# A first attention in one kernel with three other layers: transposes behind a step's four products, finishing in small pieces, value products two steps behind

## The chip, the core and the metric

One NeuronCore of a Trainium2 chip runs the whole program. Its engines work side by side, each through its own instruction stream in order: TensorE (PE: matmuls, and transposes as matmuls with an identity), VectorE (DVE), ScalarE (ACT: exponentials and copies), GpSimd (POOL) and SyncE, which starts DMAs. Products land in PSUM, from where DVE or ACT must read them. The metric is device time in microseconds: the median of the kernel's runs, 1323.51 us over three (1322.59 to 1324.91).

## The reference

Four layers follow each other on x of 1024 tokens x 256 channels, all in fp32. Each is wrapped the same way: layer norm before, layer norm behind, then added to x. Only the first, an attention of 16 heads of 16 channels, is touched.

```python
def _L0_attn_ref(X, ln_w, ln_b, W_in, W_out):
    ...
    Q, K = (_rope(Q), _rope(K))
    scores = jnp.einsum('bhqd,bhkd->bhqk', Q, K) / jnp.sqrt(jnp.float32(Dh))
    probs = jax.nn.softmax(scores, axis=-1)
    ctx = jnp.einsum('bhqk,bhkd->bhqd', probs, V)
    ctx = ctx.transpose(0, 2, 1, 3).reshape(B, S, D)
    out = jnp.einsum('bsd,df->bsf', ctx, W_out)
    return out + X
...
x = L0_attn_X
x = x + _layernorm(_L0_attn_ref(_layernorm(x, axis=-1), ...), axis=-1)
x = x + _layernorm(_L0_ffn_ref(_layernorm(x, axis=-1), ...), axis=-1)
```

The second layer is a mixture of 8 experts; a second attention and a mixture of 16 experts follow.

## The kernel before

**Tiling.** Heads come in four groups g of four; a head has a slot of 32 partitions, so the four heads of a group lie in the four 32-row strips of TensorE. Queries are taken in two halves qh of 512 tokens. The eight pairs (qh, g) are `steps`, numbered n = 0 to 7. An fp32 product runs as two passes, so every product shows as two matmul instructions.

**Two passes over the scores.** `largest` computes for every n the scores with queries in rows (L396) and reduces them on DVE to a maximum for each query and head (L401), which is written into the queries as an extra channel (L415). It has 16 positions s per n: half of the keys, a tile of 128 queries, a pair of heads. `attend(qh, g)` then computes the scores with keys in rows (L443), which come out with the maximum subtracted, takes the exponential on ACT (L472) into tiles `pe` (six buffers), and multiplies them with the values (`gather`, L437) into `po`, which has one PSUM buffer. It has eight key tiles st; each is done in two half-steps of two heads.

**How they are woven together.** `largest` and `attend` are generators. `attend` yields once in a half-step, after its first score and before its second; there the caller pulls one position of `largest`: two products, for the two heads that `attend` is not using. So the four products of a half-step lie in four row strips. After them comes half of a value product: four heads, 256 of 512 columns, of the key tile before (st - 1). In the first tile of an attend there is none; tile 0's values are taken whole at the end of tile 1, and the last tile's whole at the end of the attend, followed by an ACT copy of `po` to `oT` (L479). All score tiles, and everything that is transposed or projected, share one PSUM ring of seven buffers, tag b1. A tile waits until the one seven places earlier has been read.

**Transposes.** `turned` (L354, L355) makes four 128x128 transposes and an ACT copy. `largest` calls it at fixed positions: at s = 1 for the signed queries of n - 1 (`signed`), at s = 9 and 11 for the next group's keys (n + 1 < 4 only), at s = 13 for the next unsigned queries (`unsigned`), and at the end for the last signed queries. As it is called inside `largest`, it runs in the middle of the half-step, between `attend`'s first and second score. `pull(2 * TT + 2)` runs 18 positions ahead of the first attend, and one half-step (n = 0, i = 7) pulls three at once. So `largest` ends after 54 of the 64 key tiles. The last ten run "alone": four scores at once, four exponentials (L461), a whole value product.

**Finishing.** When n = 4 begins, the first half of the queries is finished by `finished(0)`, one step at every yield, again in the middle of a half-step: four `by_token` (four transposes L492, a reciprocal and a multiplication on DVE), two `by_channel` (transposes L507, ACT copy), two `projected` (eight matmuls L517, then on DVE L524 and all of `turn_over`: statistics, the scale with its power on POOL L184, the addition to x, statistics and scale again, then `h` on ACT L206). `turn_over` leaves `turned`, which transposes `h` (L216) and copies it to `hT` (L217), two yields later. The second half of the queries is finished by the same functions between the gates of the experts that follow (`experts0`, whose matmuls are L645). Those read `hT` of the first half of the tokens first.

The order written in the code is not fully binding: the framework may put an instruction that is ready ahead of one that is not.

Of the kernel before, what the change touches and what calls it, by code (L numbers as in the profile page):

```python
# [23 lines left out]
H = 16  # L24
# [25 lines left out]
class Net:  # L50
# [139 lines left out]

    def turn_over(self, ps, tts):

        nc = self.nc
        tp = tts[0] // 2
        xs = self.pair(self.x, tp)
        rs, nb = self.scales(self.pair(self.acc, tp))
        for i, x in enumerate(xs):
            nc.vector.scalar_tensor_tensor(  # L200
                x, self.acc[:, 2 * tp + i, :], rs[:, i : i + 1], x, ALU.mult, ALU.add
            )
        rs2, nb2 = self.scales(xs)
        h = self.row.tile([P, 2, D], F32, tag="h2", name="h")
        for i, x in enumerate(xs):
            nc.scalar.activation(  # L206
                h[:, i, :], x, AF.Identity, scale=rs2[:, i : i + 1], bias=nb2[:, i : i + 1]
            )
        for i, x in enumerate(xs):
            nc.gpsimd.tensor_scalar(x, x, nb[:, i : i + 1], None, ALU.add)  # L210

        def turned(ps):
            pt = ps.tile([P, KC, 2, P], F32, tag="b1", name="pt")
            for i in range(2):
                for k in range(KC):
                    nc.tensor.transpose(pt[:, k, i, :], h[:, i, k * P : (k + 1) * P], self.ident)  # L216
            nc.scalar.copy(  # L217
                self.hT[:, :, 2 * tp * P : (2 * tp + 2) * P], pt.rearrange("p k i t -> p k (i t)")
            )

        self.todo.extend([None, None, turned])
# [103 lines left out]
    def attention0(self):  # L325
# [4 lines left out]
        with ExitStack() as ctx:  # L330
# [49 lines left out]
            def largest(first):  # L380
# [6 lines left out]
                for n, (qh, g) in enumerate(steps):  # L387
                    raw = raws.pop(n)
                    pm = self.small.tile([P, QT, G, 2], F32, tag="pm", bufs=2, name="pm")
                    for s, (kh, tt, pair) in enumerate(order):  # L390
# [13 lines left out]
                        if s % 2 == 1:  # L404
                            next(first, None)
                        if n > 0 and s == 1:
                            signed(n - 1)
                        if n + 1 < len(steps):
                            nqh, ng = steps[n + 1]
                            if nqh == 0 and s in (9, 11):  # L410
                                turned(kT[:, ng, half((s - 9) // 2)], ng, 1, (s - 9) // 2)
                            if s == 13:
                                unsigned(n + 1)
                        if s == len(order) - 1:
                            nc.vector.tensor_reduce(  # L415
                                qk[:, qh * QT : (qh + 1) * QT, 0, g * G : (g + 1) * G, DH : DH + 1],
                                pm, AX.X, ALU.max, negate=True,
                            )
                            if n == len(steps) - 1:
                                signed(n)  # L420
                        yield

            def attend(qh, g, alone):


                qm = ready.pop((qh, g))
                po = pso.tile([P, HALF], F32, tag="po", name="po")
                NQ = HALF // 2

                def gather(st, pe, quarter, whole=False):  # L430
                    c = slice(quarter * NQ, (quarter + 1) * NQ)
                    if st == 0 or whole:
                        if quarter == 0:
                            return
                        c = slice(0, HALF)
                    for j in range(G):
                        nc.tensor.matmul(  # L437
                            po[rows(j), c], va[:, st, g * G + j, :], pe[j // 2][:, j % 2, c],
                            start=(st == 0), stop=(st == TT - 1 and quarter == 1),
                        )  # L440
# [8 lines left out]
                before = None  # L449
                for st in range(TT):  # L450
                    pe = [pp.tile([P, 2, HALF], F32, tag="pe", name="pe") for _ in range(G // 2)]
                    pairs = list(reversed(range(G // 2)))
                    if alone():

                        scs = []
                        for pair in pairs:
                            for i in range(2):
                                scs.append((pair, i, ps.tile([P, HALF], F32, tag="b1", name="sc")))
                                score(scs[-1][2], st, 2 * pair + i)
                        for pair, i, sc in scs:  # L460
                            nc.scalar.activation(pe[pair][:, i, :], sc, AF.Exp, scale=scale)  # L461
                        if before is not None:
                            gather(st - 1, before, 1, True)
                        before = pe
                        yield
                        yield
                        continue
                    for at, pair in enumerate(pairs):
                        for i in range(2):
# [3 lines left out]
                            if i == 0:  # L473
                                yield
                        if before is not None:
                            gather(st - 1, before, at)
                    before = pe
                gather(TT - 1, before, 1, True)
                nc.scalar.copy(oT[:, g, half(qh)], po)  # L479

            def finished(qh):
# [4 lines left out]
                def by_token(tp, i, ps):  # L486
                    if i == 0:
                        cxs[tp] = self.row.tile([P, 2, H, DH], F32, tag="h2", name="cx")
                    tt = 2 * tp + i
                    pt = ps.tile([P, H, SLOT], F32, tag="b1", name="pt")  # L490
                    for g in range(NG):
                        nc.tensor.transpose(  # L492
                            pt[:, g * G : (g + 1) * G, :].rearrange("p h c -> p (h c)"),
                            oT[:, g, tt * P : (tt + 1) * P], self.ident,
                        )
                    rec = self.small.tile([P, H, 1], F32, tag="rec", name="rec")
                    nc.vector.reciprocal(rec, pt[:, :, DH : DH + 1])
                    nc.vector.tensor_tensor(
                        cxs[tp][:, i, :, :], pt[:, :, 0:DH], rec.to_broadcast([P, H, DH]), ALU.mult
                    )  # L500

                def by_channel(tp, ps):
                    cx = cxs[tp].rearrange("p i h c -> p i (h c)")
                    pc = ps.tile([P, KC, 2, P], F32, tag="b1", name="pc")
                    for i in range(2):
                        for k in range(KC):
                            nc.tensor.transpose(pc[:, k, i, :], cx[:, i, k * P : (k + 1) * P], self.ident)  # L507
                    cT = self.row.tile([P, KC, 2, P], F32, tag="cT", bufs=2, name="cT")
                    nc.scalar.copy(cT, pc)
                    cxs[tp] = cT  # L510

                def projected(tp, ps):
                    cT = cxs.pop(tp)
                    po = ps.tile([P, 2, D], F32, tag="b1", name="po")
                    for i in range(2):
                        for k in range(KC):
                            nc.tensor.matmul(  # L517
                                po[:, i, :], cT[:, k, i, :], self.w_out[:, k, :],
                                start=(k == 0), stop=(k == KC - 1),
                            )  # L520

                    for i in range(2):
                        tt = 2 * tp + i
                        nc.vector.scalar_tensor_tensor(  # L524
                            self.acc[:, tt, :], self.x[:, tt, :], self.rs0[:, tt : tt + 1],
                            po[:, i, :], ALU.mult, ALU.add,
                        )
                    self.turn_over(ps, [2 * tp, 2 * tp + 1])

                for tp in tps:  # L530
                    for i in range(2):
                        yield lambda ps, tp=tp, i=i: by_token(tp, i, ps)
                for tp in tps:
                    yield lambda ps, tp=tp: by_channel(tp, ps)
                for tp in tps:
                    yield lambda ps, tp=tp: projected(tp, ps)
# [19 lines left out]
            left = [2 * TT * len(steps)]  # L556
            ahead = largest(beside())

            def pull(n):
                for _ in range(n):  # L560
                    if left[0]:
                        next(ahead)
                        left[0] -= 1

            pull(2 * TT + 2)
            after = iter(())
            for n, (qh, g) in enumerate(steps):
                if n == NG:
                    after = finished(0)
                for i, _ in enumerate(attend(qh, g, lambda: left[0] == 0)):  # L570
                    pull(3 if n == 0 and i == 7 else 1)
                    step = next(after, None)
                    if step is not None:
                        step(ps)
                    else:
                        self.catch_up(ps, 1)
            for step in after:
                step(ps)
            self.catch_up(ps, len(self.todo))
# [740 lines left out]
```

## Time and profile before

| | |
|---|---|
| median of 3 runs | 1323.51 us |
| profiled execution, its own time | 1320.31 us |
| its span, first to last instruction | 1318.5 us |
| PE busy, share of span | 94% |
| DVE, ACT, POOL busy | 55%, 38%, 11% |
| mean granted PE clock | 0.986 |
| from the first score of attend 0 to the first matmul of the experts | 69.53 to 339.06 us |

The page divides the span among engines and lists groups of instructions by source line; the trace behind it gives every instruction's start and duration. "Idle before" names whose end ended a wait. PE's busy share says little, because the passes of up to four products run at the same time in different row strips, and the end of a matmul is modelled. What counts here is the distance from one start to the next. The granted clock says at which share of its full speed PE ran.

### The profile page before, as it was taken

To read this page: it belongs to the slowest core of one execution; us is meant where nothing else is said; L and a number is where in the kernel's file an instruction comes from. 1 tells how busy PE (TensorE), PEld (TensorE's weight loads), DVE (VectorE), ACT (ScalarE), POOL (GpSimd) and SP (SyncE) were. 2 spreads that over 40 slices of the span, in tenths; PEclk is the share of its full clock that TensorE was granted. 3 is DMA by queue.
4 is the path that set the end of the run, shared out by engine and by line. 5 is a ranking of instruction groups with operands and counts; after the bars stand their busy time and mean duration, and the time that the engine had idled before them with its cause. 6 is when DMAs were issued, how large, how long until landed. Compare 5 with 4: busy or idle time off the path is not lost. (4 is left out here: it accounts for less than half of the span.)

```text
span 1318.5 us, 15710 instructions
## 1 busy us (share of the span) xinstructions
PE 1244.9 (94%) x6088; PEld 729.0 (55%) x6088; DVE 731.6 (55%) x1657; ACT 497.4 (38%) x911; POOL 149.4 (11%) x137
## 2 busy tenths in 40 slices
PE   5899999999999998889999999999998799999997
PEld 2433333332456565456676767676767456655655
DVE  4675665563243335777586777777775633233334
ACT  3256663566441111454545444445445122011111
POOL 2100000100010002111212121211112400000000
PEclk9999999899999999899999999999999899999999
DMA  6000000000005101200212112130211103723000
GB/s 189 1 1 1 1 1 1 0 1 1 1 1 172 53 12 53 83 33 32 72 33 72 50 56 72 33 103 33 73 32 34 61 1 95 218 80 108 32 25 32
DMA packets 38923, 64.42 MB, mean 49 GB/s; under 512 B 4776, under 2 KB 28552, under 8 KB 38848
## 3 DMA queue, kind: packets, MB, share of 16 engines
q1 hardware_dynamic: 38848, 63.41, 15.2%
q8 instruction: 48, 0.79, 0.3%
q14 instruction: 27, 0.22, 0.1%
HBM read 62.12 MB, written 1.28 MB: 48 GB/s over the span
## 5 line engine op out<-in xcount | busy, mean ns | idle before, releaser
L401 DVE TENSOR_REDUCE pm<-sc 128x1 f32<-128x512 f32 x256 | 163.4, 684 | 94.2 <-PE sc L443 56.5
L443 PE MATMUL sc<-qTm,kT 32*128 32x512 f32 x512 | 170.5, 644 | 2.4 <-DVE pm L401 1.7
L648 DVE TENSOR_TENSOR mid<-sg,pu 128x512 f32<-128x512 f32 (+1 forms) x82 | 56.4, 687 | 200.3 <-PE pu L645 166.7
L472 ACT ACTIVATE pe<-sc 128x512 f32<-128x512 f32 x216 | 119.1, 595 | 87.5 <-PE sc L443 59.3
L647 ACT ACTIVATE sg<-pg 128x512 f32<-128x512 f32 (+1 forms) x82 | 48.9, 596 | 270.2 <-PE pg L645 270.0
L396 PE MATMUL sc<-kT,qT 32*128 32x512 f32 x512 | 140.1, 643 | 1.7 <-ACT qT L355 1.1
L969 ACT ACTIVATE sn<-pt,shift,rs 128x128 f32<-128x128 f32 x256 | 93.6, 470 | 106.9 <-DVE shift L965 106.8
L929 PE MATMUL px<-hT,w_l1a 128*128 128x512 f32 x256 | 124.1, 597 | 4.1 <-issue 3.5
L921 DVE SCALAR_TENSOR_TENSOR y<-px,cp,y 128x1023 f32<-128x1023 f32 (+5 forms) x102 | 123.2, 1211 | 2.5 <-ACT y L915 2.5
L184 POOL TENSOR_TENSOR rs<-ve,nhalf 128x2 f32<-128x2 f32 (+1 forms) x29 | 20.8, 717 | 702.6 <-DVE ve L183 698.1
L645 PE MATMUL pg<-hT,w_l1f 128*128 128x512 f32 (+1 forms) x200 | 96.0, 603 | 0.7 <-ACT hT L217 0.7
L671 DVE TENSOR_TENSOR acc<-acc,po 128x512 f32<-128x512 f32 (+1 forms) x61 | 41.1, 674 | 99.7 <-PE po L663 99.7
L645 PE MATMUL pu<-hT,w_l1f 128*128 128x512 f32 (+1 forms) x200 | 94.6, 595 | 0.0
L663 PE MATMUL po<-w_l1f,mid 128*128 128x256 f32 (+1 forms) x400 | 87.5, 379 | 0.0
L443 PEld LDWEIGHTS sc<-qTm,kT 32*128 32x128 f32 x512 | 52.5, 185 | 63.2 <-issue 42.0
L964 POOL TENSOR_TENSOR rs<-ve,nhalf 128x8 f32<-128x8 f32 x32 | 52.4, 1638 | 299.5 <-DVE ve L963 244.7
L437 PE MATMUL po<-pe,va 128*32 128x256 f32 (+1 forms) x832 | 83.3, 444 | 1.9 <-ACT pe L461 1.2
L663 PEld LDWEIGHTS po<-w_l1f,mid 128*128 128x128 f32 (+1 forms) x400 | 76.0, 190 | 13.4 <-issue 3.3
L1063 PE MATMUL pg<-hT,w_l1a 128*128 128x512 f32 x128 | 61.9, 609 | 6.5 <-DVE og L1145 4.8
L645 PEld LDWEIGHTS pu<-hT,w_l1f 128*128 128x128 f32 (+1 forms) x200 | 38.2, 191 | 48.9 <-issue 48.7
L437 PEld LDWEIGHTS po<-pe,va 128*32 128x32 f32 x832 | 18.3, 108 | 84.6 <-issue 63.7
L645 PEld LDWEIGHTS pg<-hT,w_l1f 128*128 128x128 f32 (+1 forms) x200 | 37.9, 192 | 44.7 <-issue 43.3
(196 smaller groups left out, 1936.1 us busy)
## 6 DMA issues: line engine op xcount, KB each, us to landing
spread<-rows SPq DMA_DIRECT2D x32, 512.0 KB, 4.5
w<-w SPq DMA_DIRECT2D x16, 512.0 KB, 5.0
w_l1f<-in_e_gT SPq DMA_DIRECT2D x4, 640.0 KB, 4.0
w_l1f<-in_e_uT SPq DMA_DIRECT2D x4, 640.0 KB, 5.3
w_l1f<-in_e_dT SPq DMA_DIRECT2D x4, 640.0 KB, 7.2
w_l0f<-in_e_wg SPq DMA_DIRECT2D x4, 512.0 KB, 3.7
w_l0f<-in_e_wu SPq DMA_DIRECT2D x4, 512.0 KB, 5.8
w_l0f<-in_e_wd SPq DMA_DIRECT2D x4, 512.0 KB, 6.7
```

The lines of the kernel that those rows point to most:

```text
L396: nc.tensor.matmul(sc, raw[r, tt * P : (tt + 1) * P], kT[r, g, half(kh)], start=True, stop=True,)
L401: nc.vector.tensor_reduce(pm[:, tt, 2 * pair + i, kh : kh + 1], sc, AX.X, ALU.max)
L437: nc.tensor.matmul(po[rows(j), c], va[:, st, g * G + j, :], pe[j // 2][:, j % 2, c], start=(st == 0), stop=(st == TT - 1 and quarter == 1),)
L443: nc.tensor.matmul(sc, kT[rows(j), g, st * P : (st + 1) * P], qm[rows(j), :], start=True, stop=True,)
L472: nc.scalar.activation(pe[pair][:, i, :], sc, AF.Exp, scale=scale)
L645: nc.tensor.matmul(p, w(k), self.hT[:, k, c], start=(k == 0), stop=(k == KC - 1))
L648: nc.vector.tensor_tensor(mid, sg, pu, ALU.mult)
L663: nc.tensor.matmul(po[:, i, :], left[:, at * P : (at + 1) * P], right, start=(n == 0), stop=(n == len(pieces) - 1),)
L921: nc.vector.scalar_tensor_tensor(y[:, at:hi], px[:, at - j : hi - j], column(cw + 4 * h + 3 - j), y[:, at:hi], ALU.mult, ALU.add,)
L929: nc.tensor.matmul(px[:, c], w[:, k, hh * DK : (hh + 1) * DK], self.hT[:, k, c], start=(k == 0), stop=(k == KC - 1),)
L969: nc.scalar.activation(sn[:, n, :], pts[n // 4][:, n % 4, :], AF.Identity, scale=rs[:, n : n + 1], bias=shift[:, n : n + 1],)
L1063: nc.tensor.matmul(pg, wg[:, k, hh * DK : (hh + 1) * DK], self.hT[:, k, c], start=(k == 0), stop=(k == KC - 1),)
```

## The change

Three things change in the first attention. A pull now returns what is to be transposed instead of doing it, and the caller runs it at the end of the half-step, behind the second score and the value product. The value products go into a list `sums` that outlives an attend: a half-step takes one entry while more than two are in it, so that they run two key tiles behind, across the borders between attends. Tile 0's whole product takes two entries, the first of them empty. The finishing of the first query half becomes a generator of small pieces, `finished_slowly` with `turn_over_slowly`, advanced once at the end of every half-step, from seven half-steps into n = 4 on. The pull of three at once is gone; 20 positions are pulled ahead of the first attend. `finished(1)` stays, but its projection now takes the two token tiles one after the other, each followed by its DVE instruction.

```diff
+    def turn_over_slowly(self, ps, tp, acc):
...
+        mv = small("mv", 2)
+        for i in range(2):
+            acc(i)
+            yield
+            stats(mv, i, accs[i])
+            yield
+        rs, nb = scale(mv)
+        yield
+        mv = small("mv", 2)
+        for i, x in enumerate(xs):
+            nc.vector.scalar_tensor_tensor(x, accs[i], rs[:, i : i + 1], x, ALU.mult, ALU.add)
+            yield
+            stats(mv, i, x)
+            yield
+        rs2, nb2 = scale(mv)
+        h = self.row.tile([P, 2, D], F32, tag="h2", name="h")
+        for i, x in enumerate(xs):
+            nc.scalar.activation(
+                h[:, i, :], x, AF.Identity, scale=rs2[:, i : i + 1], bias=nb2[:, i : i + 1]
+            )
+            yield
+        for i, x in enumerate(xs):
+            nc.gpsimd.tensor_scalar(x, x, nb[:, i : i + 1], None, ALU.add)
+        self.turn(ps, h, tp)
+        yield
...
+                        then = None
                         if n > 0 and s == 1:
-                            signed(n - 1)
+                            then = lambda n=n: signed(n - 1)
...
-                        yield
+                        yield then
+
+            sums = []
+
+            def gather(n):
+
+                while sums and n > 0:
+                    if len(sums) > 1 and n > 1 and sums[0][0] is sums[1][0]:
+                        sums.pop(0)
+                        sums.pop(0)[0](slice(0, HALF))
+                        n -= 2
+                        continue
+                    do, c = sums.pop(0)
+                    if c is not None:
+                        do(c)
+                    n -= 1
...
+                    if st == 0:
+                        sums.extend([(None, None), (do, slice(0, HALF))])
+                    else:
+                        sums.extend((do, slice(i * HALF // 2, (i + 1) * HALF // 2)) for i in range(2))
...
+                    for pair in pairs:
+                        pe[pair] = pp.tile([P, 2, HALF], F32, tag="pe", name="pe")
                         for i in range(2):
                             sc = ps.tile([P, HALF], F32, tag="b1", name="sc")
                             score(sc, st, 2 * pair + i)
                             nc.scalar.activation(pe[pair][:, i, :], sc, AF.Exp, scale=scale)
                             if i == 0:
-                                yield
-                        if before is not None:
-                            gather(st - 1, before, at)
-                    before = pe
-                gather(TT - 1, before, 1, True)
-                nc.scalar.copy(oT[:, g, half(qh)], po)
+                                yield True
+                        if len(sums) > 2:
+                            gather(1)
+                        if pair == pairs[-1]:
+                            summed(st, pe)
+                        yield False
+
+            def finished_slowly():
+
+                for _ in range(6):
+                    yield
+                for tp in range(QT // 2):
+                    cx = self.row.tile([P, 2, H, DH], F32, tag="h2", name="cx")
+                    for i in range(2):
+                        tt = 2 * tp + i
+                        by_token(tt, cx[:, i, :, :], ps)
+                        yield
+                        yield
+                    cT = by_channel(cx, ps)
+                    yield
+                    yield
+
+                    def acc(i):
+                        po = ps.tile([P, D], F32, tag="b1", name="po")
+                        projected(2 * tp + i, cT[:, :, i, :], po)
+
+                    for _ in self.turn_over_slowly(ps, tp, acc):
+                        yield
+                        yield
...
-            pull(2 * TT + 2)
+            while pulled < 2 * TT + 4:
+                then = pull()
+                if then:
+                    then()
             after = iter(())
             for n, (qh, g) in enumerate(steps):
                 if n == NG:
-                    after = finished(0)
-                for i, _ in enumerate(attend(qh, g, lambda: left[0] == 0)):
-                    pull(3 if n == 0 and i == 7 else 1)
-                    step = next(after, None)
-                    if step is not None:
-                        step(ps)
-                    else:
-                        self.catch_up(ps, 1)
-            for step in after:
-                step(ps)
-            self.catch_up(ps, len(self.todo))
+                    after = finished_slowly()
+                then = None
+                for inside in attend(qh, g, lambda: pulled == count):
+                    if inside:
+                        then = pull()
+                        continue
+                    if then:
+                        then()
+                        then = None
+                    next(after, None)
+            gather(len(sums))
+            for _ in after:
+                pass
             self.todo.extend(finished(1))
```

In the alone tiles `gather(len(sums))` follows the four exponentials, and both pieces of a tile come behind it. `finished_slowly` comes to 66 yields; n = 4 to 7 offer 64 half-steps. The last transpose of `h` falls behind the last value product.

## The prediction

> **What bounds the kernel now.** The chain that ended last starts far behind the first attention, so I read this stage by windows of the trace: one row for each attend, cut at the value product that closes it.
>
> ```profile
> 103.90:138.17 34.27, 34.27 (x258) 11.96 (x257) 20.62 (x34) 20.70 (x38) 0.00 (x0) 1.00 0.00 1
> 138.17:169.59 31.42, 31.42 (x250) 10.96 (x249) 20.62 (x34) 19.31 (x36) 0.00 (x0) 1.00 0.01 1
> 169.59:201.01 31.42, 31.42 (x250) 10.97 (x249) 20.62 (x34) 19.31 (x36) 0.00 (x0) 1.00 0.01 1
> 201.01:256.54 55.53, 53.24 (x297) 19.59 (x296) 30.77 (x74) 23.63 (x44) 6.47 (x8) 0.91 0.00 1
> 256.54:288.02 31.48, 31.48 (x249) 10.96 (x249) 20.67 (x34) 19.37 (x36) 0.00 (x0) 1.00 0.01 1
> ```
>
> Columns: stretch and length, busy time of PE, weight load, DVE, ACT, POOL, then granted clock and DMA. PE is busy throughout; DVE and ACT fill two thirds. PE's order sets the time. An attend with two transposes takes 31.42 us, one with four 34.27 (1.43 more for each). The fourth row, with the finishing, takes 55.53, at a clock of 0.91.
>
> The timeline of PE, a normal half-step and one with a transpose (start, length, line):
>
> ```profile
> 152.79 0.64 PE L437 MATMUL po<-pe,va 128*32 128x256 f32 x8
> 153.36 0.69 PE L443 MATMUL sc<-qTm,kT 32*128 32x512 f32 x1
> 153.37 0.70 PE L396 MATMUL sc<-kT,qT 32*128 32x512 f32 x2
> ...
> 154.43 0.64 PE L437 MATMUL po<-pe,va 128*32 128x256 f32 x8
> ...
> 155.00 0.70 PE L396 MATMUL sc<-kT,qT 32*128 32x512 f32 x2
> ...
> 156.06 0.66 PE L354 MATMUL pt<-ident,qk 128*128 128x128 f32 x4
> 156.65 1.12 PE L443 MATMUL sc<-qTm,kT 32*128 32x512 f32 x2
> 157.70 0.64 PE L437 MATMUL po<-pe,va 128*32 128x256 f32 x8
> ```
>
> Value product to value product is 1.64 us (152.79 to 154.43): 0.57 of values, 1.07 for four products side by side. With a transpose it is 3.27 (154.43 to 157.70): 0.57, then 1.06 for only three products, 0.59 of transposes, and 1.05 for the fourth product **alone**. That last 1.05 is what being in the middle costs.
>
> Every second normal half-step takes 1.85 (147.45 to 149.30). Its second score starts 0.22 late (148.25 for 148.03): its place in the ring is that of the first score of the half-step before, whose exponential started only at 147.60. So two half-steps take 3.49.
>
> **1. Transposes of `largest`, attends 1 to 6.** 4+2+2+2+2+1 = 13 are moved. A half-step then takes 1.64 or 1.85, plus 0.59: 2.23 or 2.44 for 3.27. The transposed half-steps stand where the late second score would fall (after 1.85, 1.64), so I take the lower gain, 0.83: 13 x 0.83 = **10.8** (ends 10.8 and 13.5). The ACT copy of 0.59 lies beside PE: two exponentials (1.09) and it are 1.68 of 2.23.
>
> A page speaks against this: the Trainium skill, "TensorEngine Tiling (Array Packing)", PSUM Bottleneck, says that tiling speeds TensorE but not the reading of PSUM, which then may bound. The rows: where four half-steps have no values (140.17 to 145.39) DVE works without a pause and each takes 1.30. With values PE needs 1.64 and DVE 1.29. Were reading the bound in a transposed half-step, DVE's and ACT's reads one after the other, it would take 1.29 + 1.68 = 2.97, and the 13 would bring 3.9. The rows have the two side by side (reduction at 156.20, exponential at 156.16), so I keep 10.8.
>
> **2. Attend 0.** Two more transposes: 1.7. The half-step with three pulls took 5.07 (82.04 to 87.11) and becomes 1.64 + 2 x 0.59 = 2.82: 2.25 gained. Two pulls now run ahead of the attend, on DVE's time (2 x 1.29 = 2.6), and push it back; but PE waits for DVE there anyway (four half-steps take 7.02 from 69.53). Ends 0 and 3.5 (two half-steps of 1.75), near the lower: 1.2. Sum **2.7**.
>
> **3. Borders.** The closing value product and the four half-steps after it:
>
> ```profile
> 138.17 2.08 PE L437 MATMUL po<-pe,va 128*32 128x256 f32 x16
> 140.17 0.69 PE L443 MATMUL sc<-qTm,kT 32*128 32x512 f32 x1
> ...
> 145.39 1.06 PE L437 MATMUL po<-pe,va 128*32 128x512 f32 x8
> ```
>
> The first group takes 2.00, of which 0.57 + 1.07 is work and 0.36 waits for exponentials just issued. Then come 5.22 without values at DVE's pace. To 147.45 it is 9.28 for five half-steps. Afterwards values go on across the border; only one half-step is empty and the next takes a whole product: 2 x 1.3 + 1.06 = 3.7, with three of 1.64, 1.85, 1.64 that is 8.8: 0.45 gained (ends 0.1 and 1.1), six times **2.7**. The border inside the alone tiles: six of them take 15.03 us (313.62 to 328.65) where the regular ones take 2.16 (324.33 to 335.05 by five), 12.96: **2.1** gained. Given back: the first attend starts with values two tiles late, and the first alone tile does two whole products, **1.1** more. Six `pe` buffers suffice: the first exponential of tile st + 3 reuses a buffer read by the values at the end of st + 2, which PE has run 1.2 us before.
>
> **4. Finishing.** 55.53 - 31.42 = 24.1 us now. Every step there splits a half-step, and all of a pair's statistics stand in DVE's queue ahead of the reductions that free the ring:
>
> ```profile
> 236.22 1.12 PE L443 MATMUL sc<-qTm,kT 32*128 32x512 f32 x2 [1.69 <-DVE pm L401]
> ```
>
> ```profile
> 238.00:239.00 1.00, 1.00 (x7) 0.47 (x4) 1.00 (x2) 1.00 (x3) 0.39 (x1) 0.50 0.00 0
> ```
>
> PE stands for 1.69 us, and from 237.3 to 247.9 its clock is 0.50. In small pieces: eight groups of four transposes at 0.59 (4.7), two projections at 1.93 (3.9). DVE per two half-steps: 2 x 1.29 and one piece of at most 0.65, 3.2 of PE's 3.5: beside it. Four scales hold DVE 0.8 us each for POOL; a reduction has some 0.8 of slack before the ring asks for it: 0.3 each for three, 0.9. The first `h` stands in ACT's queue behind such a scale: 1.42 for reductions, 0.97 + 0.2 to the start of `h`, 0.55 of `h`. The next exponential starts 1.4 us late, and so does a second score: 1.5. The other pair's `h` falls into the alone tiles, where ACT (2.06 a tile) is nearly as full as PE (2.14): 0.6. Sum 11.6; gained **12.5** (ends 8 and 15).
>
> The last transpose of `h` now stands between the last value product and the experts, which read its copy: 0.59 of PE (counted above) and the copy behind that of `oT`, some 1.37 from value product to L645 where it was 0.76. No more is lost than the 0.59 counted.
>
> The clock is a second place for a rule. The skill, "TensorE: Matmul & The Clock Gate", HAM oscillation, puts the fall to half clock behind an idle gap of about 3.4 us. Here it fell with no gap above 1.69, so the measurement decides: thin work suffices. By the rule no piece of mine could bring it back. By the row the wait for `h` is the candidate, at some 0.55 us of empty PE in 3 us of thin work; I take it as too short. If it fell, 10.6 us at half speed cost 5.3.
>
> **5. The other half's finishing.** In `finished(1)` a second projection writes the PSUM tile that DVE is just reading (0.48). No row shows whether it waits: 0 to 1.4 (two pairs, 0.7 each), taken at **0.6** lost, since gates of the experts may stand between.
>
> **Sum.** 10.8 + 2.7 + 2.7 + 2.1 - 1.1 + 12.5 - 0.6 = **29.1 us**. The profiled execution took 1320.3 (span 1318.5 and 1.8 around it) and would take 1291.2. The median of the runs lies 3.2 above it: 1323.5 - 29.1 = **1294.4**. Nothing behind the experts' first matmul is touched but in its start.
>
> **Rivals.**
>
> A, *half a gain*: the finishing is only moved. ACT and DVE pieces meet the ring's wait (late second scores become the rule while pieces run: 64 half-steps x 0.1 = 6.4) and the clock falls once more (5.3). 29.1 - 11.7 = 17.4: 1306. For it: POOL and ACT waits of 0.8 to 4.7 us in the old finishing. Against it: they came from eight DVE instructions in one block.
>
> B, *more*: the 0.22 vanishes too. Transposes and pieces behind the values give the exponential more cover than 0.57, and about 40 late scores x 0.21 = 8.4: 1286. Against it: most half-steps still have only the values as cover.
>
> C, *slower*: three key tiles now hold all six `pe` buffers. If the value product that frees one is placed later than written, every tile's first exponential waits on PE, and a late exponential delays a second score by as much. There are 54 such tiles; from 29.1 / 54 = 0.54 us of waiting in each the gain is gone, and at 0.8 the kernel takes 1323.5 + 54 x 0.8 - 29.1 = 1338. For it: between 309.40 and 313.62 the trace has a value product ahead of a score that the code puts first, and PE waiting. Against: 1.2 us of slack.
>
> D, *it doesn't do what it says*: the scheduler puts ready transposes back in the middle. Then 1. and part of 2. go: 29.1 - 10.8 - 3 = 15: 1308. In the trace of before the transposes stand where the code has them.
>
> **Chances.** Forecast 1294.4 (1289 to 1300): 0.56. A 0.18, D 0.06, B 0.15, C 0.05. The range, 1284 to 1308, holds all but C and the edges of A, B and D. The bounds alone (13.5 for 10.8, 15 or 8 for 12.5, 1.1 or 0.1 at borders) reach from 1284 to 1302. Two runs of this kernel can be told apart from about 0.2%, 2.6 us: faster 0.94, same 0.01, slower 0.05.
>
> **What would show it.** Half-steps with L354 should last 2.2 to 2.45 us from values to values, with no L443 pair alone behind them; else step 1 is wrong. An attend with two transposes should take about 29.3 us. The border should show 0.64-us value groups right into the next attend. The clock should be 1.00 through the finishing, and attends 4 to 6 should exceed 29.3 by some 10 together. ACT's wait for `nb` should show once at about 1.4 us. Waits of L472 on L437 would speak for C. Wrong altogether if PE shows new idle time of tens of us.

## The result and the profile after

The changed kernel takes 1303.28 us (median of four runs, 1301.19 to 1308.75), the kernel before 1324.21 in the same series: a ratio of 0.9847, interval 0.9812 to 0.9882. That is 20.9 us gained where 29.1 were forecast. In the two profiled executions the stage from the last but one group of passes in the preparation (the same four, at 67.14 and 68.27 us) to the experts' first matmul went from 271.9 to 251.2 us: 20.7 gained, in this stage alone. The span fell by 18.0 only: the stage began 1.1 later (the clock stood at 0.53 from 55 to 60 us in that execution, and at 1.00 in that of the kernel before), and 1.6 were lost behind it.

The rows of the windows view for the changed kernel, for attend 2 (from its first value product to that of attend 3, which takes the same 29.50), and then for two stretches of about an attend's length from the first value product of attend 4 on. The columns are those of the prediction:

```profile
144.07:173.57 29.50, 29.50 (x258) 10.17 (x257) 20.70 (x34) 19.02 (x35) 0.00 (x0) 1.00 0.00 1
...
203.07:233.09 30.02, 30.01 (x253) 10.89 (x252) 21.79 (x45) 15.98 (x29) 0.71 (x1) 1.00 0.01 1
233.09:265.87 32.78, 31.57 (x243) 10.93 (x240) 21.06 (x36) 19.40 (x36) 2.53 (x3) 0.90 0.00 1
```

An attend with two transposes takes 29.50 us for 31.42. The last row is the first sign of trouble: PE idles for 1.2 us and its granted clock is 0.90. The timeline of PE around a transposed half-step and, further on, a border:

```profile
87.22 0.64 PE L500 MATMUL po<-pe,va 128*32 128x256 f32 x8
87.79 0.66 PE L402 MATMUL pt<-ident,qk 128*128 128x128 f32 x4
...
89.45 0.64 PE L500 MATMUL po<-pe,va 128*32 128x256 f32 x8
...
109.91 0.64 PE L500 MATMUL po<-pe,va 128*32 128x256 f32 x8
...
113.39 1.06 PE L500 MATMUL po<-pe,va 128*32 128x512 f32 x8
```

The transposes follow the values, no product stands alone, and the half-step lasts 2.23 us (87.22 to 89.45) for 3.27. At the border small value groups run on to 109.91, and one half-step is empty.

What is missing went in two places. The first, from the timeline (idle time before an instruction in brackets, with what ended it):

```profile
231.98 0.45 DVE L221 SCALAR_TENSOR_TENSOR x<-acc,rs,x 128x256 f32<-128x256 f32 x1
...
234.12 0.16 DVE L208 SCALAR_TENSOR_TENSOR nb<-mv,rs 128x2 f32<-128x2 f32 x1 [0.81 <-POOL rs L207]
234.20 3.78 DVE L449 TENSOR_REDUCE pm<-sc 128x1 f32<-128x512 f32 x6
234.32 1.09 ACT L228 ACTIVATE h<-x,nb,rs 128x256 f32<-128x256 f32 x2 [3.27 <-DVE nb L208]
...
234.94 1.12 PE L513 MATMUL sc<-qTm,kT 32*128 32x512 f32 x2 [1.21 <-DVE pm L449]
```

The code sets a pair's pieces two half-steps apart. Here the second addition to x, its statistics and the scale stand on DVE close behind one another (231.98 to 234.12), ahead of six reductions that then run without a pause. ACT waits 3.27 us with both `h` (L228, x2) at the head of its queue and the exponentials behind them. The scheduler has put the pieces' DVE and ACT instructions ahead of the ones that feed the ring (e3 and e4 below test this). PE waits 1.21 us. Then the clock falls (windows view):

```profile
234.00:236.00 2.00, 1.06 (x4) 0.64 (x5) 1.88 (x5) 1.68 (x4) 1.07 (x3) 1.00 0.00 0
236.00:238.00 2.00, 2.00 (x13) 1.33 (x11) 1.97 (x4) 1.98 (x5) 0.85 (x1) 0.79 0.00 0
238.00:240.00 2.00, 2.00 (x9) 0.50 (x10) 1.13 (x2) 0.94 (x3) 0.00 (x0) 0.50 0.00 0
```

The second place, in the alone tiles:

```profile
297.96 0.16 DVE L208 SCALAR_TENSOR_TENSOR nb<-mv,rs 128x2 f32<-128x2 f32 x1 [0.81 <-POOL rs L207]
298.15 0.60 ACT L228 ACTIVATE h<-x,nb,rs 128x256 f32<-128x256 f32 x1 [2.07 <-DVE nb L208]
298.66 0.56 ACT L505 COPY oT<-po 128x512 f32<-128x512 f32 x1
...
299.28 1.93 PE L500 MATMUL po<-pe,va 128*32 128x512 f32 x8 [3.27 <-ACT oT L505]
```

An `h` waits 2.07 us in ACT's queue for its `nb`, and behind it waits the copy of `po` to `oT` (L505). `po` has one buffer, so the next attend's first value product waits for that copy: PE stands 3.27 us. The clock is 0.50 from 298.60 to 305.42, and in the first place from 237.16 to 243.98. Both stretches last 6.83 us, so each lacks 3.4 us' worth of clock.

### The profile page after: what moved, and what is told of

It reads as the page before. It is cut to its first block, busy times and chain, and to the rows that moved or that the text cites. A ratio compares the mean times of both kernels' runs of the same rounds, so it can differ in the third digit from the quotient of the medians.

```text
span 1300.5 us, 15783 instructions
## 1 busy us (share of the span) xinstructions
PE 1222.9 (94%) x6128; PEld 723.0 (56%) x6128; DVE 733.0 (56%) x1657; ACT 495.6 (38%) x911; POOL 149.1 (11%) x137
## 4 chain that ended last, share of the span: by engine, by line
PE 36%; DVE 9%; ACT 3%; POOL 2%; DMA 2%; issue 1%; POOLq 0%; SPq 0%; DVEq 0%
PE po L764 10%; PE pg L746 7%; PE pu L746 7%; PE px L1030 3%; DVE st L1051 2%; PE pg L1164 2%; DMA spread<-rows 2%; POOL rs L1065 2%; PE pv L1100 2%; PE psc L1212 2%; DVE dec L1152 1%; PE pkv L1220 1%; PE pt L1078 1%; DVE state L1229 1%; ACT sn L1070 1%
## 5 line engine op out<-in xcount | busy, mean ns | idle before, releaser
L513 PE MATMUL sc<-qTm,kT 32*128 32x512 f32 x512 | 152.7, 654 | 2.1 <-DVE pm L449 2.1
L444 PE MATMUL sc<-kT,qT 32*128 32x512 f32 x512 | 139.2, 659 | 1.7 <-ACT qT L403 1.1
L513 PEld LDWEIGHTS sc<-qTm,kT 32*128 32x128 f32 x512 | 49.5, 188 | 54.8 <-issue 41.8
L184 POOL TENSOR_TENSOR rs<-ve,nhalf 128x2 f32<-128x2 f32 (+1 forms) x25 | 17.5, 701 | 463.6 <-DVE ve L183 459.1
```

The costliest lines, as they stand in the source:

```text
L444: nc.tensor.matmul(sc, raw[r, tt * P : (tt + 1) * P], kT[r, g, half(kh)], start=True, stop=True,)
L513: nc.tensor.matmul(sc, kT[rows(j), g, st * P : (st + 1) * P], qm[rows(j), :], start=True, stop=True,)
```

## Experiments

Where kernels with the changed structure are compared, the stage is measured from attend 0's first value product to the experts' first matmul, since the clock ahead of it differs between executions. Each stage is read from one profiled execution. It was 236.8 us in the changed kernel.

**e1, the transposes alone**, in the kernel before (cut to the core):

```diff
-                            signed(n - 1)
+                            then = lambda n=n: signed(n - 1)
...
-                        yield
+                        yield then
...
                         if before is not None:
                             gather(st - 1, before, at)
+                        yield False
```

> The kernel of before with one part of the change: the transposes of largest run behind the half-step's value product; value products, borders, the three-fold pull and the finishing in the middle of half-steps are as before. My theory: a transposed half-step falls from 3.27 us (values to values) to 2.23 or 2.44 by this alone, whatever the value products do: 16 transposes x 0.83 + about 1 for the half-step with three pulls = 13 to 15 us less, about 1309.5 us; an attend with two transposes takes 29.7 instead of 31.42. Rival (the gain in the attends comes from values two tiles behind, since a value product one tile behind has to wait for exponentials once the half-step is shorter): less than 8 us.

1314.11 us, ratio 0.9914 (0.9883 to 0.9945): 10.4 us less than the kernel before, and 10.3 in the stage. An attend with two transposes took 29.75 us. So the transposes bring 0.83 each with the values still one tile behind: nothing waits there. The attend with the old finishing did not improve (56.5 us for 55.5), and that is why the whole is 10 and not 13 or more as expected.

**e2, no finishing of the first query half** (left out altogether):

```diff
-                if n == NG:
-                    after = finished_slowly()
```

> The changed kernel without the finishing of the first query half (attention output, projection, layer norm and transposes of tokens 0 to 511 are left out, so what follows works on other data). If the two places where PE stood (at 234 and 296 us) and the half clock behind them are what my sum missed, then the finishing costs 8.6 us of PE work and about 12 us of waits and half clock: 20 us less than the changed kernel, about 1283 us, with the clock at 1.00 all through the attends. If the pieces cost what the prediction said (11.6 us), about 1291.5 us.

1288.12 us (1281.43 to 1290.45), ratio 0.9707 (0.9658 to 0.9755); the stage is 217.9 us. So the finishing in small pieces costs 236.8 - 217.9 = 18.9 us (the expectation had about 20), of which 8.6 are PE's own work by the prediction's count. The prediction had 11.6 in all.

**e3 and e4, the pieces kept in order.** e3 asks the scheduler to issue a piece behind the last exponential or `oT` copy written ahead of it; e4 also behind the last reduction:

```diff
-                    next(after, None)
+                    with tc.issue_after(last["DVE"].ins), tc.issue_after(last["ACT"].ins):
+                        next(after, None)
```

> The changed kernel; the only edit is that each piece's ACT instructions may not be issued ahead of the exponentials and the oT copy that the code puts before them. Theory: the 3.3 us in which PE waits for the oT copy behind h at 296 us, and the half clock that follows, vanish: 5 to 6 us less than the changed kernel, about 1297.5 us, while the stall at 234 us stays. Rival (the oT copy is late for another reason, or PE's thin work in the alone tiles lowers the clock anyway): within 2 us of the changed kernel.

> As the run before, and each piece's DVE instructions too may not be issued ahead of the reductions that the code puts before them. Theory: the statistics and scales of both token tiles, now all within 227 to 234 us and ahead of six reductions, go back to one piece in two half-steps; the stall at 234 us and the half clock behind it vanish as well: 10 to 12 us less than the changed kernel, about 1292 us, near the 1294.4 of the prediction. Rival (a scale that waits for POOL stops PE wherever it stands): the gain over the run before is under 2 us and the clock still falls.

e3: 1296.46 us (1292.53 to 1300.81), ratio 0.9778 (0.9736 to 0.982). e4: 1294.34 us (1291.65 to 1296.71), ratio 0.976 (0.9728 to 0.9793). The stages are 229.3 and 226.9: ACT's order brings 7.5 of the 18.9, DVE's 2.4 more, and 9.0 are left, which is PE's work and 0.4. In e3 the second place is gone and the first still there, with `h` no longer in front (timeline, then windows):

```profile
235.63 0.16 DVE L208 SCALAR_TENSOR_TENSOR nb<-mv,rs 128x2 f32<-128x2 f32 x1 [0.81 <-POOL rs L207]
235.70 3.78 DVE L449 TENSOR_REDUCE pm<-sc 128x1 f32<-128x512 f32 x6
...
236.44 1.12 PE L514 MATMUL sc<-qTm,kT 32*128 32x512 f32 x2 [1.21 <-DVE pm L449]
```

```profile
238.00:240.00 2.00, 2.00 (x11) 0.77 (x7) 1.47 (x3) 1.04 (x3) 0.00 (x0) 0.53 0.00 0
240.00:242.00 2.00, 2.00 (x15) 0.31 (x13) 1.29 (x2) 1.01 (x2) 0.00 (x0) 0.61 0.00 0
```

The six reductions stand in a row behind the scale, as before, and the clock falls for half as long: it is 0.50 from 238.13 to 241.55, 3.41 us. In e4 it doesn't (windows over an attend that holds pieces, then the timeline of the one late half-step):

```profile
232.50:264.50 32.00, 31.92 (x274) 11.33 (x276) 23.49 (x46) 21.37 (x40) 3.26 (x4) 1.00 0.00 1
```

```profile
255.48 0.16 DVE L208 SCALAR_TENSOR_TENSOR nb<-mv,rs 128x2 f32<-128x2 f32 x1 [0.81 <-POOL rs L207]
...
255.68 0.60 ACT L228 ACTIVATE h<-x,nb,rs 128x256 f32<-128x256 f32 x1 [1.27 <-DVE nb L208]
```

This is the wait for the first `h` that the prediction priced at 1.5 us; ACT waits 1.27, and the half-step takes 2.84 us (255.02 to 257.86).

The next four all start from e4.

**e5, values one tile behind within an attend:** `gather(1)` without its condition `len(sums) > 2`.

> Base: the kernel with every piece held in its place (1294.3 us). Edit: a half-step always takes an entry of sums, so value products run one key tile behind, still across the borders. My theory: the second tile of delay buys nothing, since a value product one tile behind asks for exponentials that end 1.25 to 1.35 us after the scores that PE left 1.64 us before; and the first attend starts its values two half-steps earlier: 0 to 1.5 us less than the base, about 1293.5 us. Rival (the delay is what keeps PE from waiting for exponentials now that half-steps are short): over 3 us more, with waits of L500 on the exponential.

1294.63 us (1292.81 to 1301.54), ratio 0.9777 (0.9733 to 0.9822). Half-steps are 1.64 and 1.85 as in e4, and from the preparation's passes named above the stage is 241.5 us for 240.7. The second tile of distance makes less than a microsecond of difference.

**e6, values closed at the end of every attend:**

```diff
                         next(after, None)
+                gather(len(sums))
```

> Base: the kernel with every piece held in its place (1294.3 us). Edit: all value products left over are done at the end of each attend, so none crosses a border. Expected from the prediction's terms: 2.1 us lost at the border in the alone tiles, 0.24 (measured on the changed kernel, 9.04 for 9.28) to 0.45 lost at each of the six others, and up to half a us more for each, as two tiles are left over instead of one: 4 to 6 us more than the base. Rival (the borders cost nothing, because exponentials and reductions catch up there): within 1.5 us of the base.

The expectation missed. 1294.26 us (1290.3 to 1298.86), ratio 0.9766 (0.9722 to 0.981), stage 225.3 us, 1.6 less than e4: an attend with two transposes took 28.84 us (its first value product at 172.27, the next one's at 201.11) for the 29.50 with values across the border. The timeline of a border:

```profile
162.47 2.36 PE L501 MATMUL po<-pe,va 128*32 128x256 f32 x24
...
165.95 7.48 DVE L449 TENSOR_REDUCE pm<-sc 128x1 f32<-128x512 f32 x12 [2.27 <-PE sc L514]
```

The values left over, five halves of a tile, are done in one block, from 162.47 to the next score at 164.75: 2.28 us. Spread over half-steps, as in e4, each half takes 0.57 from its start to the next product, five of them 2.85. That is 0.57 of the 0.66 gained. DVE then reduces twelve tiles without a pause: six half-steps at 1.25. So crossing doesn't save the work of the values, and it cuts it into dearer pieces. Only between the two attends of the alone tiles did closing lose: one tile there took 4.12 us (286.42 to 290.54), about twice the usual 2.07.

**e7, `h` one piece behind its scale** (and two empty yields fewer ahead):

```diff
         rs2, nb2 = scale(mv)
+        yield
         h = self.row.tile([P, 2, D], F32, tag="h2", name="h")
...
-                for _ in range(6):
+                for _ in range(4):
```

> Base: the kernel with every piece held in its place (1294.3 us). Edit: the first h is a piece of its own, two half-steps behind the scale that it waits for, and the pieces start two half-steps earlier to make room. In the base one half-step holds that pair and takes 2.84 us from values to values where 1.64 is regular (255.02 to 257.86). Theory: ACT's wait for nb, with the exponentials queued behind it, is that 1.2 us: about 1 us less than the base, no half-step of 2.8. Rival (the half-step is late because of DVE's reductions behind the scale): the 2.8 stays.

1297.61 us (1296.02 to 1298.97), ratio 0.9794 (0.975 to 0.9837), stage 230.5: 3.6 more than e4, against the expectation. The 2.84 half-step is gone (1.75, 1.68 and 1.81 there). But the generator now has 4 + 2 x 32 = 68 yields for 64 half-steps. The second `h` of the second pair is the 65th piece, and the loop that empties the generator behind the last half-step has no `issue_after`. One `h` runs free ahead of the `oT` copy, while the other stays at 310.35:

```profile
291.58 0.60 ACT L229 ACTIVATE h<-x,nb,rs 128x256 f32<-128x256 f32 x1 [2.07 <-DVE nb L208]
292.09 0.56 ACT L507 COPY oT<-po 128x512 f32<-128x512 f32 x1
...
292.70 1.93 PE L502 MATMUL po<-pe,va 128*32 128x512 f32 x8 [3.27 <-ACT oT L507]
```

It is the second place again, with the same 2.07 and 3.27 us and again 6.83 us at half clock (291.86 to 298.69). An `h` that isn't pinned brings it back in a kernel in which the rest is. So the order of these two instructions is the cause, and not something else that e3 changed.

**e8, e7 with one empty yield fewer after each `by_token` and each `by_channel`**: all pieces now fit into the half-steps, so both `h` are pinned, and the last transpose comes ahead of the last value products.

> The run before, with one empty half-step less behind the second by_token and behind by_channel, so that the last transpose of h and its copy stand ahead of the last value products instead of between them and the experts. Theory: 0.6 us less (1.33 from transpose to L746 becomes some 0.7, of which the transposes' 0.6 go into an alone tile that ACT nearly fills): about 1292.5 us. Rival: the denser pieces meet the ring's wait and it is no faster.

1296.69 us (1292.69 to 1301.0), ratio 0.9784 (0.9741 to 0.9826). The stage is 225.5 us, 5.0 less than e7 and 1.4 less than e4: no collision, and no tail of transposes. By its median it can't be told from e4 or e7.

**e9 to e11**, in one series of five rounds: e4 once more, e4 with the values closed in attends 0 to 5 only, and e8 with the same:

```diff
+                if n < 6:
+                    gather(len(sums))
```

> The kernel of e4 once more, beside e10 and e11, so that the three can be compared with each other. From its stage (240.7 us from the first pass of the last value projection to the experts' first matmul, 31.2 less than before) both theories expect about 1293 us.

> As e4, but the values are closed at the end of attends 0 to 5, and cross the border only between the two attends that hold the alone tiles. My theory after e6: at the borders beside the maxima, crossing costs 0.66 us each (half-steps without values run at DVE's pace of 1.30 and catch up), in the alone tiles closing costs about 2 us. So the stage should be 240.7 - 6 x 0.66 = 236.7 us or, from e6's 239.3 less the 2 at the alone border, 237.3; the time 3.5 to 4 us below e9, about 1290. The rival, that e6's shorter attends only moved time to its later ones, expects e9's time within 1 us.

> As e8 (pieces in order, h apart from its scale, the last transpose ahead of the last value products), with the values closed at the end of attends 0 to 5 as in e10. My theory: e8's stage of 239.6 less 4.0 is 235.6 us, about 1 below e10. The rival: closing moves the pieces against the reductions again, and the order of h and the oT copy costs about 5 us more, as in e7.

| | median, us | ratio to before (interval) | stage, us |
|---|---|---|---|
| e9 | 1296.53 (1292.16 to 1306.91) | 0.9801 (0.9767 to 0.9834) | 226.9 |
| e10 | 1290.83 (1289.62 to 1295.16) | 0.9751 (0.9726 to 0.9775) | 224.6 |
| e11 | 1292.58 (1288.16 to 1295.30) | 0.9760 (0.9736 to 0.9785) | 223.3 |

e9 is e4's kernel once more. Its stage repeats e4's to 0.03 us, while its median is 2.2 higher and the two profiled executions differ by 4.6 (1296.71 and 1292.16). That scatter lies outside the stage, so stages can show what medians can't. e10 gains 2.3 us in the stage, not 3.5 to 4, and e11 2.2 on e8, not 4.0. Between first value products, attends 0 to 3 gain 0.65 or 0.66 each as in e6; attend 4, which holds pieces, gains 0.37, and attend 5 loses 0.69 (31.79 us for 31.10). So neither side was right: where no pieces run the gain stays, and the finishing takes part of it back. From e6 to e10, which differ in the border of the alone tiles alone, the stage fell by 0.7 us: that is what crossing is worth there. Among the kernels that do the whole work, e10 has the lowest median and e11 the shortest stage; their order is open, since the intervals overlap. Both intervals lie below that of the changed kernel.

## Why the prediction held in direction and missed in size

**The step that failed is 4, the finishing**, with its claim that the pieces run "beside it" and its "I take it as too short" for the clock. It was to cost 11.6 us and cost 18.9 (e2). The prediction took each piece where the code writes it, one to two half-steps. It had named "the scheduler puts ready transposes back in the middle" as rival D, but for PE alone; on DVE and ACT the scheduler did move instructions, and there each waits in order with all that stands behind it. Kept in order, the same pieces cost 9.0 (e4), less than the forecast, although the wait for the first `h` is there as priced: PE's 8.6 and this wait are together more than 9.0, so the scales and the second `h` cost next to nothing, and pieces fill places where a late second score stood: in e4 three half-steps with transposes in a row take 2.23, 2.23 and 2.22 us. Of the 9.9 us between 18.9 and 9.0, the clock's share is some 6.8, twice the half of 6.83; this is worked out, no run held the clock and left the waits. So rival A's clock term came true, and twice; its other half (late second scores as the rule while pieces run) did not.

**Step 1, right.** Transposed half-steps take 2.22 to 2.23 us, as 0.57 + 0.59 + 1.07; 1.04 gained, and in half the cases given back in part because the next half-step keeps the late second score (1.85): net 0.83, as taken. e1 shows it by itself. Reading of PSUM did not bound these half-steps: that would have made them 2.97.

**Step 2, not shown by itself.** From the preparation's passes named above to the first score of attend 1 it was 38.77 us (67.14 to 105.91) and is 35.23 (68.27 to 103.50). That is 3.54 gained for the 2.7, but the values of two key tiles, four halves at 0.57, are only put off there.

**Step 3, nearly twice too high, and the wrong design.** Five half-steps at a border take 9.04 for 9.28: 0.24 gained, not 0.45. e6 and e10 show that closing there is 0.66 better still, so the crossing pays only in the alone tiles, and there 0.7 us (e6 to e10), where step 3 had 2.1. At the six other borders the term was small, and so was its error: six times 0.21, 1.3 us.

**Step 5, wrong in the other direction.** From the experts' first matmul to their next one behind the other half's projections it is 19.92 us in both kernels (339.06 to 358.98, 319.51 to 339.43): none of the 0.6 was lost. The tail is 1.33 us from the last transpose of `h` to the experts, of which 0.68 is PE's wait for the copy; 1.37 were forecast.

**The other rivals.** B is wrong in the main: the late second score stays at 0.21 us (1.85 for 1.64) wherever no pieces stand, and only between pieces does it shrink (1.79) or vanish. C is wrong: no exponential waited for a value product (in attends 1 to 3 they wait for their scores, 18.0 us by L513 and 10.4 by L444), and e5, which holds its `pe` for a shorter time, is no faster.

In sum: 29.1 forecast, less 7.3 for the finishing and 1.3 for the borders, plus 0.6, is 21.1; the stage shows 20.7. That the two are so near is in part luck, since step 2 and the terms of the alone tiles stand in this sum as forecast.

## What to carry to other kernels

Pieces woven into a loop have to be followed on every engine's queue, not only on the one that bounds: an instruction that is ready early, or one that waits for a slow neighbour, stands in front of whatever feeds the ring. Ask of each added wait what is behind it in its own queue (here an `oT` copy with one `po` buffer behind an `h`), and pin the order against the last instruction that must come first, in every loop that issues pieces (e7 missed one). Small work cut to fit into gaps can cost more than the same work in one block, as the values at the borders did. When the rest of a stage repeats to hundredths, compare stages in the trace rather than medians.

## What the runs showed of the hardware

The clock fell to half after a PE wait of only 1.21 us, in work that had been thin for some 3 us (PE busy 1.06 of the 2 us from 234 to 236), and stayed there for 6.83 us; behind 3.27 us of waiting it took as long. In e3 the same wait of 1.21 cost 3.41 us at half clock. In the kernel before it was 10.24 us (237.67 to 247.91; the prediction read 10.6). In the preparation, ahead of all that the change touches, the same kernel ran at half clock for 10.24 us in e4 (53.59 to 63.83) and not at all in e9, and e10's profiled execution for 27.31 us (52.24 to 79.55). Every stretch named here is 3.41 us long or 2, 3 or 8 times that. So a spell of thin work cost half speed in steps of 3.41 us, and each step takes up to 1.7 us of PE's work, the half of it. Why the same wait of 1.21 brought two steps in the changed kernel and one in e3 stays open.
